# The first batch of a two-layer graph kernel: products of ones during the first loads, conv1 half by half, messages later, three x parts ahead of the way back

## The chip, the cores and the metric

The kernel runs on one core of a Trainium2 chip. The metric is the device time of one execution in microseconds (us), as a median over runs. PE is TensorE, PEld its weight load, DVE is VectorE, ACT is ScalarE, POOL is GpSimd. "L461" is a line of the kernel; the change shifts lines, so L461 of before is L465 of after, L380 is L384, L396 is L400, L521 is L538, L555 is L573, L693 is L711.

## The reference, cut to what matters

64 graphs of 256 nodes and 256 features go through two layers; all is float32.

```python
# layer 0, per graph
h = relu(bn1(conv1d(xT, conv1_w)))              # 1x1 convolution over the nodes
h = bn2(conv1d(h, conv2_w, pad=8))              # 17 taps along the nodes
x_conv = relu(h + xT).T
s = x @ w_se.T + b_se                           # 3 numbers a node
A = exp(-|s_n - s_m|^2) * adj
msg = relu(x @ w_msg.T + b_msg)
x_in = concat([x_conv, A @ msg])
# GRU: gates from x_in @ w_ih.T and x @ w_hh.T, then x = layernorm(x + gru)
# layer 1: x = layernorm(x + relu(adj @ layernorm(x) @ W_rel + ... @ W_root))
```

## The kernel before, where the change touches it

Eight graphs make a batch. While the graphs of batch b go through gates and layer 1, the convolution of batch b+1 runs in between. The first batch has nothing before it, so its convolution stands alone: conv1, building the filters, a tree of VectorE adds, eight groups of products (TensorE) with a "take" each (VectorE), and the "way back", 20 VectorE steps whose result TensorE turns. Then the first gates can start.

Some words recur. A pair is two graphs; a batch has pairs 0 to 3. The profile counts each f32 matmul as two instructions, called passes. "Turned" means transposed by TensorE. An x part is a quarter of turned x that TensorE leaves in PSUM, for a quarter of the way back to be added to it. Messages, factors, distances, mask and passing are, for one graph, the steps to A @ msg: the message matmul, the turned s, the exponential of the distances, its product with adj, and the product with the messages. A gate matmul belongs to the GRU. The clock is the share of TensorE's full speed that the profile says was granted.

```python
for g in range(0, BG, 2):                       # conv1, two graphs at a time
    xTc = conv_pool.tile([P, C, 2 * N], F32, tag="xTc", name="xTc", bufs=1)
    ...                                         # 8 transposes, 2 ScalarE copies into xTc
    nc.scalar.dma_start(out=xt_dram[pair], in_=xTc)     # the write of turned x
    for o in range(C):
        ps = bank("ps_c1")
        for c in range(C):
            nc.tensor.matmul(ps, w1[:, c, o * P:(o + 1) * P], xTc[:, c, :], ...)
...
held = [turned_x(0), turned_x(1)]               # two x parts before the way back
... for q in range(4):                          # way back, by quarters
        second(q); third(q); third(q + 4)       # VectorE
        pss = held.pop(0)                       # TensorE adds the quarter to its x part
        ...
        if q < 2: held.append(turned_x(q + 2))
...
while STAGE.get(0) != "inverse":
    if next(first) is None:                     # a product group is done
        count += 1
        if count == 2:   messages(0, True)
        elif count == 3: messages(1, True)
        elif count == 4: factors(0)
        elif count == 5: distances(0)
...
nc.gpsimd.tensor_add(brzn[:, :2 * D], brzn[:, :2 * D], bhh)
early = {1: lambda: messages(2, True), 4: lambda: mask(0), 5: lambda: factors(1)}
later = deque([lambda: distances(1), lambda: passing(0)])
```

`bank` hands out the eight PSUM banks in a ring. `xTc` has one buffer, so the copies of a pair wait until the write of the pair before has landed.

## Time and profile before

| | value |
|---|---|
| time, median of 3 runs | 2287.5 us (2286.13 to 2288.14) |
| span of the profiled run | 2289.9 us (that run took 2291.63) |
| PE busy | 2228.0 us, 97% |
| products begin (first L380) | 80.39 |
| last VectorE step of the way back ends | 157.04 |
| first gate matmul (L693) | 164.61 |

The profiled run was itself 4 us above the median.

```profile
19.87 1.07 ACT L453 COPY xTc<-ps_xTc 128x512 f32<-128x512 f32 x2 [0.15 <-DMA xt<-xTc]
```

The first pair of graphs takes 4.50 us instead of 3.70, because its first passes run at half clock. The views show a granted clock of 1.00 there, but the list of clock intervals in the packed trace begins only at 10.67, with an interval at full clock, and has nothing before it. That agrees with the spacing of the weight loads, which the prediction reads as a switch near 10.6.

### The profile page before, as it was taken

To read this page: it belongs to the slowest core of one execution; us is meant where nothing else is said; L and a number is where in the kernel's file an instruction comes from. 1 tells how busy PE (TensorE), PEld (TensorE's weight loads), DVE (VectorE), ACT (ScalarE), POOL (GpSimd) and SP (SyncE) were. 2 spreads that over 40 slices of the span, in tenths; PEclk is the share of its full clock that TensorE was granted. 3 is DMA by queue.
4 is the path that set the end of the run, shared out by engine and by line. 5 is a ranking of instruction groups with operands and counts; after the bars stand their busy time and mean duration, and the time that the engine had idled before them with its cause. 6 is when DMAs were issued, how large, how long until landed. Compare 5 with 4: busy or idle time off the path is not lost.

```text
span 2289.9 us, 24427 instructions
## 1 busy us (share of the span) xinstructions
PE 2228.0 (97%) x8370; PEld 1463.0 (64%) x8370; DVE 1678.3 (73%) x3188; ACT 768.1 (34%) x1585; POOL 464.0 (20%) x926
## 2 busy tenths in 40 slices
PE   8989999999999999999999999999999999999996
PEld 5765666666665666656666566666666566666663
DVE  6875979478882988749886597947888398874443
ACT  6423222432234322443224422243223432243332
POOL 0101212221220221213022121222122022121211
PEclk9989999999999999999999999999999999999998
DMA  5922432314422153232422243231442315321100
GB/s 146 312 92 74 130 119 83 101 51 138 134 74 101 39 170 99 75 101 93 146 85 76 83 129 120 82 102 51 138 133 74 102 39 163 102 79 37 47 23 14
DMA packets 212665, 226.68 MB, mean 99 GB/s; under 512 B 22087, under 2 KB 203838, under 8 KB 212542
## 3 DMA queue, kind: packets, MB, share of 16 engines
q1 hardware_dynamic: 189984, 191.14, 26.1%
q10 hardware_dynamic: 22558, 33.99, 4.3%
q8 instruction: 67, 1.10, 0.2%
q14 instruction: 56, 0.46, 0.1%
HBM read 179.22 MB, written 45.88 MB: 98 GB/s over the span
## 4 chain that ended last, share of the span: by engine, by line
PE 79%; DVE 14%; DMA 3%; issue 2%; POOL 1%; ACT 1%; SPq 0%; ACTq 0%; POOLq 0%; DVEq 0%
PE ps_rz L695 16%; PE ps_k L380 12%; PE ps_n L707 8%; PE ps_rz L693 8%; PE ps_out L770 7%; PE ps_c L461 5%; DVE XF L103 5%; PE ps_nmp L677 5%; PE ps_n L705 4%; PE ps_msg L627 4%; PE ps_out L782 4%; DMA w<-w2m 2%; PE ps_w L225 2%; DVE w L103 1%; DVE bst L712 1%
## 5 line engine op out<-in xcount | busy, mean ns | idle before, releaser
L103 DVE SCALAR_TENSOR_TENSOR XF<-XF 128x512 f32<-128x512 f32 (+2 forms) x800 | 508.2, 665 | 7.4
L734 POOL TENSOR_SCALAR q<-mv 128x2 f32<-128x2 f32 x64 | 32.1, 501 | 1473.6 <-DVE mv L713 1473.6
L380 PE MATMUL ps_k<-w,XF 128*128 128x256 f32 x1316 | 304.5, 387 | 15.9 <-ACT AT L667 11.6
L380 PEld LDWEIGHTS ps_k<-w,XF 128*128 128x128 f32 x1316 | 249.4, 192 | 65.6 <-ACT AT L667 17.3
L708 DVE TENSOR_TENSOR gn<-ps_n,brzn 128x512 f32<-128x512 f32 x128 | 87.9, 687 | 239.9 <-PE ps_n L707 239.9
L699 ACT ACTIVATE rz<-rz 128x512 f32<-128x512 f32 x128 | 80.7, 631 | 507.1 <-DVE rz L698 507.1
L693 PE MATMUL ps_rz<-whh,xT 128*128 128x512 f32 x512 | 240.8, 592 | 0.0
L695 PE MATMUL ps_rz<-wih,nmp 128*128 128x512 f32 x512 | 240.6, 592 | 0.0
L695 PE MATMUL ps_rz<-wih,xc 128*128 128x512 f32 x512 | 240.6, 592 | 0.0
L770 PE MATMUL ps_out<-wrr,hT 128*128 128x512 f32 x512 | 231.8, 596 | 5.5 <-ACT hT L759 5.5
L698 DVE TENSOR_TENSOR rz<-ps_rz,brzn 128x512 f32<-128x512 f32 x128 | 87.1, 680 | 199.9 <-PE ps_rz L695 199.8
L695 PEld LDWEIGHTS ps_rz<-wih,xc 128*128 128x128 f32 x512 | 97.3, 190 | 122.5 <-issue 122.2
L695 PEld LDWEIGHTS ps_rz<-wih,nmp 128*128 128x128 f32 x512 | 97.3, 190 | 122.4 <-issue 122.4
L770 PEld LDWEIGHTS ps_out<-wrr,hT 128*128 128x128 f32 x512 | 97.8, 191 | 104.5 <-issue 88.9
L638 ACT ACTIVATE msg<-msg 128x512 f32<-128x512 f32 x61 | 38.5, 631 | 335.1 <-DVE msg L636 335.1
L627 PE MATMUL ps_msg<-wms,xT 128*128 128x260 f32 x512 | 133.2, 399 | 5.8 <-DVE XF L396 4.2
L693 PEld LDWEIGHTS ps_rz<-whh,xT 128*128 128x128 f32 x512 | 92.2, 190 | 64.5 <-issue 61.2
L705 PE MATMUL ps_n<-whh,xT 128*128 128x256 f32 x512 | 131.6, 379 | 0.0
L707 PE MATMUL ps_n<-wih,nmp 128*128 128x256 f32 x512 | 131.4, 379 | 0.0
L707 PE MATMUL ps_n<-wih,xc 128*128 128x256 f32 x512 | 131.4, 379 | 0.0
L357 DVE TENSOR_TENSOR XF<-XF 128x512 f32<-128x512 f32 (+3 forms) x128 | 125.2, 1003 | 1.7
L771 ACT COPY hr<-ps_out 128x256 f32<-128x256 f32 x128 | 47.7, 373 | 229.9 <-PE ps_out L770 229.9
(115 smaller groups left out, 3556.1 us busy)
## 6 DMA issues: line engine op xcount, KB each, us to landing
w<-w2m SPq DMA_DIRECT2D x105, 768.0 KB, 5.8
xn<-in_x_dram SPq DMA_DIRECT2D x32, 512.0 KB, 4.4
xt<-xTc ACTq DMA_DIRECT2D x32, 512.0 KB, 3.2
xT<-xt SPq DMA_DIRECT2D x64, 256.0 KB, 2.9
xb<-in_x_dram SPq DMA_DIRECT2D x32, 512.0 KB, 5.3
adj<-in_adjT_dram SPq DMA_DIRECT2D x64, 256.0 KB, 2.7
x<-in_x_dram SPq DMA_DIRECT2D x64, 256.0 KB, 3.0
out_dram<-y ACTq DMA_DIRECT2D x64, 256.0 KB, 2.2
```

Of the source, the lines that this page charges most:

```text
L103: nc.vector.scalar_tensor_tensor(o, in0, s, in1, op0=op0, op1=op1)
L357: (nc.vector.tensor_add if add else nc.vector.tensor_sub)(sl(o, n), sl(a, n), sl(b, n))
L380: nc.tensor.matmul(ps, X[:, slot, c * P:(c + 1) * P], w(m, c), start=(c == 0), stop=(c == C - 1))
L461: nc.tensor.matmul(ps, w1[:, c, o * P:(o + 1) * P], xTc[:, c, :], start=(c == 0), stop=(c == C - 1))
L627: nc.tensor.matmul(ps[:, :D + 4], XT[k][:, c, m * P:(m + 1) * P], wms[:, c, :], start=(c == 0), stop=(c == C - 1 and not idle))
L677: nc.tensor.matmul(ps[:, d * N:(d + 1) * N], MSG[k][:, m, d * P:(d + 1) * P], AT[k][:, m, :], start=(m == 0), stop=(m == C - 1))
L693: nc.tensor.matmul(prz, XT[k][:, c, q], whh[:, c, 0:2 * D], start=(c == 0), stop=False)
L695: nc.tensor.matmul(prz, t, wih[:, i, 0:2 * D], start=False, stop=(i == 3))
L705: nc.tensor.matmul(pn[:, D:], XT[k][:, c, q], whh[:, c, 2 * D:], start=(c == 0), stop=(c == C - 1))
L707: nc.tensor.matmul(pn[:, :D], t, wih[:, i, 2 * D:], start=(i == 0), stop=(i == 3))
L770: nc.tensor.matmul(ps, hT[:, c, n * P:(n + 1) * P], wrr[:, c, :], start=(c == 0), stop=(c == C - 1))
L782: nc.tensor.matmul(po, ADJ[k][:, m, n * P:(n + 1) * P], hr[:, m, :], start=False, stop=(m == C - 1), skip_group_check=True)
```

## The change

The intent is to shorten the first 165 us: let TensorE reach full clock during the first loads, use each half of x as it lands, keep messages out of the way of the product group that VectorE waits for, and put work into the stretch in which VectorE alone decides.

```diff
+    warm = bank("ps_warm")
+    for _ in range(8):
+        nc.tensor.matmul(warm[:, :P], ones, ones, start=True, stop=True)
 ... conv1
+            if b == 0:
+                pss = [bank("ps_c1") for _ in range(C)]
+                for c in range(C):
+                    for o in range(C):
+                        product1(o, c)           # half of x outermost
 ... way back
-            held = [turned_x(0), turned_x(1)]
+            yield None
+            held = [turned_x(q) for q in range(3)]
-                if q < 2:
-                    held.append(turned_x(q + 2))
+                if q == 1:
+                    held.append(turned_x(3))
 ... product groups of batch 0
-            if count == 2:                       # messages(0); 3: messages(1); 4: factors(0); 5: distances(0)
+            if count == 3:                       # 4: messages(1); 5: factors(0); 6: distances(0)
+    messages(2, True)
-    early = {1: lambda: messages(2, True), 4: lambda: mask(0), 5: lambda: factors(1)}
-    later = deque([lambda: distances(1), lambda: passing(0)])
+    early = {2: lambda: factors(1), 3: lambda: mask(0), 4: lambda: passing(0)}
+    distances(1)                                 # after the way back
```

More of the change, by code (lines that the diff above doesn't have):

```diff
@@ L457, in conv, with product1 @@
             yield None
-            for o in range(C):
-                ps = bank("ps_c1")
-                for c in range(C):
-                    nc.tensor.matmul(ps, w1[:, c, o * P:(o + 1) * P], xTc[:, c, :], start=(c == 0), stop=(c == C - 1))
+            pss = []
+            def product1(o, c):
+                nc.tensor.matmul(pss[o], w1[:, c, o * P:(o + 1) * P], xTc[:, c, :], start=(c == 0), stop=(c == C - 1))
+            if b == 0:
[3 more added lines that the diff above has]
+                        product1(o, c)
+            for o in range(C):
+                if b > 0:
+                    pss.append(bank("ps_c1"))
+                    for c in range(C):
+                        product1(o, c)
+                ps = pss[o]
                 pv = ps.rearrange("p (g t j) -> p j g t", g=2, j=M)
@@ L888, in gnn_two_layers @@
             count += 1
-            if count == 2:
+            if count == 3:
                 messages(0, True)
-            elif count == 3:
+            elif count == 4:
                 messages(1, True)
-            elif count == 4:
+            elif count == 5:
                 factors(0)
-            elif count == 5:
+            elif count == 6:
                 distances(0)
+    messages(2, True)
     first_pool.close()
@@ L906, in gnn_two_layers @@
     load_x(0)
-    early = {1: lambda: messages(2, True), 4: lambda: mask(0), 5: lambda: factors(1)}
-    later = deque([lambda: distances(1), lambda: passing(0)])
-    for i, t in enumerate(first):
+    early = {2: lambda: factors(1), 3: lambda: mask(0), 4: lambda: passing(0)}
+    for i, _ in enumerate(first):
         if i in early:
             early[i]()
-        if t is None and later:
-            later.popleft()()
+    distances(1)
     mask(1)
```

## The prediction

> **What bounds the kernel now.** The page first: TensorE is busy 97% of a 2289.9 us span and carries 79% of the chain that ended last. The second view, the busy time by slices of the first 200 us, shows where it is not busy; only there can a change to the first batch gain anything.
>
> ```profile
> PE 2228.0 (97%) x8370; PEld 1463.0 (64%) x8370; DVE 1678.3 (73%) x3188; ACT 768.1 (34%) x1585; POOL 464.0 (20%) x926
> ```
>
> ```profile
> 0.00:10.00 10.00, 5.00 (x18) 4.14 (x19) 2.40 (x14) 3.04 (x4) 3.04 (x13) 1.00 0.90 231
> ...
> 130.00:140.00 10.00, 7.13 (x41) 5.67 (x39) 9.69 (x18) 0.37 (x1) 0.00 (x0) 0.85 0.82 255
> 140.00:150.00 10.00, 5.64 (x15) 3.18 (x15) 9.73 (x15) 1.72 (x6) 4.34 (x7) 0.50 0.69 217
> 150.00:160.00 10.00, 10.00 (x68) 9.47 (x68) 7.47 (x12) 4.92 (x10) 0.32 (x1) 0.80 0.01 2
> ```
>
> The columns after the window's length are PE, PEld, DVE, ACT, POOL, then granted PE clock, DMA share, GB/s. The first 200 us hold 16.9 us of TensorE's 62 idle us, in two places: the start (5 us with nothing to do), and 130 to 150 us, the "way back" of the first batch's convolution. There VectorE is full (9.7 of 10) and TensorE waits for it, at half clock for part of it.
>
> Third view, TensorE's own timeline from 84 us (start, duration, instructions, idle before):
>
> ```profile
> 92.26 1.11 PE L627 MATMUL ps_msg<-wms,xT 128*128 128x260 f32 x4 [1.11 <-issue]
> ...
> 104.23 5.45 PE L380 MATMUL ps_k<-w2all,XF 128*128 128x256 f32 x24
> 109.51 0.38 PE L653 MATMUL ps_sT<-ident,st 128*36 128x128 f32 x2
> ...
> 136.13 1.34 PE L521 MATMUL ps_xc<-ident,xb 128*128 128x128 f32 x8 [2.87 <-DVE XF L396]
> ...
> 148.53 3.96 PE L555 MATMUL ps_xc<-ident,XF 128*128 128x128 f32 x16 [3.82 <-DVE XF L103]
> 152.28 2.79 PE L521 MATMUL ps_xc<-ident,xb 128*128 128x128 f32 x16
> ...
> 161.04 3.73 PE L555 MATMUL ps_xc<-ident,XF 128*128 128x128 f32 x32
> 164.61 1.88 PE L693 MATMUL ps_rz<-whh,xT 128*128 128x512 f32 x4
> ```
>
> And VectorE's, same stretch:
>
> ```profile
> 101.19 0.69 DVE L396 TENSOR_TENSOR XF<-XF,ps_k 128x512 f32<-128x512 f32 x1 [1.68 <-PE ps_k L380]
> ...
> 109.78 0.69 DVE L396 TENSOR_TENSOR XF<-XF,ps_k 128x512 f32<-128x512 f32 x1 [5.06 <-PE ps_k L380]
> ...
> 145.14 11.90 DVE L103 SCALAR_TENSOR_TENSOR XF<-XF 128x512 f32<-128x512 f32 x18
> ```
>
> Read together: up to 109.78 VectorE waits for TensorE (5.06 us) because two message steps stand between product groups. From 109.78 on it never waits until its last way-back step ends at 157.04 (145.14 + 11.90): 47.3 us of unbroken work. TensorE then still has 7.6 us queued before the first gate matmul at 164.61. So the path is TensorE to 109.7, VectorE to 157.0, TensorE after that; from 164.6 on TensorE is nearly full to the end, so what is gained before it should reach the end whole. The printed chain hangs the stretch from 133 on a DMA; VectorE was busy all through it, so I do not follow the chain there.
>
> **What the Trainium skill says.** "TensorE: Matmul & The Clock Gate", Part 1: the array starts and falls back to half clock, and goes to full clock only after a busy window of about 3.4 us, free-running, so the switch moves from run to run. The trace agrees: the weight loads of the first L461 are 0.86 us apart (8.85, 9.71, 10.56), then 0.43, so the switch came near 10.6, 5.6 us after the first matmul (the recorded clock reads 1.00 there, which the spacing contradicts); the clock fell to 0.50 at 137.0 after a 2.87 us gap, and came back at 154.0, 17.0 us later, five windows of 3.4. The same page, "Why this matters for your kernels", advises no gaps above about 3 us. "SBUF — State Buffer", "Who interferes with whom": VectorE reading two SBUF operands and a GpSimd read lock each other out. The trace agrees: one L103 step at 142.87 took 1.75 us against 0.69 for its neighbours while GpSimd's L905 add ran 142.39 to 144.07. That add stays. "PSUM — Partial Sum Buffer", "The four PSUM rules": eight banks; three x parts held in advance take six, so later users wait for a bank's reader.
>
> **The change part by part.**
>
> (1) Eight products of ones. Added: 8 matmuls 128x128 f32, two passes each. A cold pass of 128 columns is 0.21 us: L461's cold pass of 512 columns takes 0.86, a quarter of that. So 16 x 0.21 = 3.4 us. They wait only for the memset of ones (ends 1.02), so they run 1.1 to 4.5, before the first x lands at 4.86 (the chain has that load 0.73 + 4.14): they cost nothing. Gain: with 0.4 us of pause the clock should rise at a window edge in about 4.5 to 8 us instead of 10.6. L461 of the first pair then saves its two slow steps, 0.86 us; L161 is partly held by VectorE's dg tiles and saves about 0.5. Sum 1.4. It may be damped by DMA, which is full to 18.6 us and whose xt write at 15.41 took 4.38 and releases the tile of pair 2.
>
> (2) conv1 half by half. Same matmuls. The first half's result is complete after the third matmul, not the second, so ScalarE's two evictions start 0.86 later; they end just as the second half's could start (2.57 + 0.2 + 1.0 against 3.43 + 0.2). In before the second matmul never waited for the second copy (copies 0.5 apart, matmul 0.86). So it buys nothing and may cost 0.07 a pair, 0.2 in all. With the damping I take 1.1 net for (1) and (2).
>
> (3) Messages later. Messages(0) moves from after product group 1 to after group 2, messages(1) after group 3, messages(2) after group 7. The 1.11 us before messages(0) is its xT load (issued from 83.35, 7.0 us to land): one group later, 5.4 us, it is there, gain 1.1. And only one message step (92.26 to 95.64, 3.3 us) is left before the end of group 3, which releases VectorE at 109.78. So that release moves by 1.1 + 1.1 + 3.3 = 5.5, to 104.3. VectorE is free by then: group 2's take, now at about 98.3 (its merges end 99.51 - 1.1), plus the 3.5 us from 101.19 to 104.72, gives 101.8. Later takes are never ahead of their groups: groups 4 to 7 end by about 112.7, 118, 123.8, 128.4, the takes come at 119, 122.6, 129.9, 133.3. VectorE's end: 157.04 - 5.5 = 151.5.
>
> (4) Three x parts ahead, passing(0) before, distances(1) after the way back. In before, after VectorE's end TensorE still ran part of its queue to 164.61, 7.6 us. Now TensorE ends the products at 128.4, messages(2) at 131.7, three x parts (48 passes x 0.107 = 5.2) at 136.9, and passing(0) once mask(0) is done (137.4) at 139.1. It then waits to 143.0 (148.5 - 5.5) for the first quarter: 3.9 us, enough for the clock to fall. From there a quarter is ready each 2.85 us (148.5 to 157.04 in three). Work: two quarters, the fourth x part, two quarters, distances: 5 x 1.75 + 0.63 warm. Never cold: 151.5 + 1.75 + 0.63 = 153.9. Cold for 3.4 to 6.8 us: 154.3 to 155.6. I take 154.7. From VectorE's end to the gates is then 3.2 instead of 7.6: gain 4.4. ScalarE's relu of the last quarter (four of 0.46) ends about 156, when the whh gate matmuls (1.72) have just run: no stall.
>
> Sum: 1.1 + 1.1 + 3.3 + 4.4 = 9.9 us; first gate matmul at 154.7 instead of 164.6; 2287.5 - 9.9 = 2277.6.
>
> **Rivals.** (a) The clock rules: if the warm products do not lift it (the windows may need more than 88% busy), part 1 gives 0; a bad phase in the way back costs 1 more. Total gain 7.5 to 8.5: 2279 to 2280. For: in before a window about two thirds busy did not lift it. (b) The later work comes due elsewhere: passing(1), distances(1) or loads become the wait after 155, since adjacency, wih and x start only 2.2 us earlier (they wait for the last product) while the gates start 9.9 earlier. Against: wih landed about 8.5 us after its issue, at 140.6; now about 138.5, with the gates at 156; and pair loads have 10 us of room. If half is lost: 2282. (c) The bank ring: the second half of the third x part waits for the take of group 7 (about 133.5, needed 136), the fourth x part for the readers of passing and factors. Small room, but none on VectorE's path; at worst 1 us. (d) More: before also loses to cold windows in 137 to 154, and if TensorE keeps its clock the gain is nearer 11.5: 2276.
>
> **Range and chances.** The terms are uncertain by about 0.8, 0.3, 0.5 and 1.2, and two executions of one kernel differ by 2 us here[...]. So 2272.5 to 2282.5. 2% is 46 us, more than the whole idle time of the first 200 us, so faster by 2% is out of reach; slower would need a stall that the order does not show.
>
> **What would show it.** Right: L461's weight loads 0.43 apart from the first pair; no 1.1 us gap before messages(0); VectorE's 5.06 us wait cut to about 2.5 and its way back ending near 151.5; the first L693 near 154.7; from there equal spacing. Wrong: L461 still 0.86 apart; VectorE waiting inside 104 to 151; a gap of several us before the gates' wih matmuls; or a first gate at 155 with an end that moved less.

## More of the kernel before

The views that bound the kernel stand in the prediction. Two more matter later: TensorE's timeline of conv1 (start, duration, instructions, and in brackets the idle time before them with what ended it) and one line of ScalarE's.

```profile
8.85 4.50 PE L461 MATMUL ps_c<-xTc,w 128*128 128x512 f32 x8
...
14.94 3.70 PE L461 MATMUL ps_c<-xTc,w 128*128 128x512 f32 x8 [0.71 <-ACT xTc L453]
...
20.51 3.70 PE L461 MATMUL ps_c<-xTc,w 128*128 128x512 f32 x8 [0.99 <-ACT xTc L453]
```

The copies of pair 2 waited only 0.15 us for the write of turned x: the write was just about hidden.

## The result and the profile after

The changed kernel took 2278.97 us (median of 6 runs, 2275.36 to 2282.39); the kernel before took 2287.49 (6 runs, 2285.87 to 2288.14) in the same rounds. The ratio is 0.9964, 95% interval 0.9951 to 0.9977. A ratio is the mean time of one kernel's runs over that of the other's of the same rounds, so it is not quite the ratio of the medians. The outputs were correct.

The page's line of engines, and the busy times by slices in the form that the prediction uses (after the length: PE, PEld, DVE, ACT, POOL, granted PE clock, DMA share, GB/s):

```profile
PE 2224.9 (98%) x8386; PEld 1462.9 (64%) x8386; DVE 1678.0 (74%) x3188; ACT 766.9 (34%) x1585; POOL 467.1 (20%) x926
```

```profile
0.00:10.00 10.00, 8.10 (x35) 6.71 (x36) 2.35 (x14) 3.04 (x4) 3.04 (x13) 1.00 0.89 224
130.00:140.00 10.00, 10.00 (x68) 8.21 (x67) 9.69 (x20) 1.98 (x7) 1.78 (x5) 1.00 0.89 280
140.00:150.00 10.00, 6.59 (x30) 6.06 (x29) 9.79 (x15) 2.87 (x6) 1.63 (x2) 0.66 0.60 195
150.00:160.00 10.00, 10.00 (x68) 7.87 (x67) 3.31 (x6) 6.27 (x14) 0.32 (x1) 1.00 0.18 52
```

TensorE is now full from 130 to 140 (before 7.13) at full clock (before 0.85), and VectorE is done at the beginning of the last slice, where it was still busy before. From 140 to 150 the clock is low again. Next, TensorE's timeline of the start, and ScalarE's line that goes with it:

```profile
1.07 3.79 PE L136 MATMUL ps_warm<-ones 128*128 128x128 f32 x16 [1.07 <-DVE ones L132]
...
8.79 3.60 PE L465 MATMUL ps_c<-xTc,w 128*128 128x512 f32 x8
...
14.03 3.70 PE L465 MATMUL ps_c<-xTc,w 128*128 128x512 f32 x8 [0.76 <-ACT xTc L457]
...
20.62 3.70 PE L465 MATMUL ps_c<-xTc,w 128*128 128x512 f32 x8 [2.02 <-ACT xTc L457]
```

```profile
19.98 1.07 ACT L457 COPY xTc<-ps_xTc 128x512 f32<-128x512 f32 x2 [1.14 <-DMA xt<-xTc]
```

The products of ones lie where they were meant to, and the first pair runs at full clock (3.60 instead of 4.50), so pair 1 starts 0.91 us earlier. The list of clock intervals begins at 6.59 here; it begins at 3.98 to 7.29 in all ten profiles with the ones and at 10.08 to 12.53 in the four without. But the copies of pair 2 now wait 1.14 us for the write of turned x, and pair 2 starts at 20.62, where before it started at 20.51: all is given back. The first pair did not even begin earlier (8.79 against 8.85), because the small load of the norm factors, on which the row products ahead of it hang, landed at 4.12 instead of 3.41. Now the middle and the end, TensorE first and then VectorE:

```profile
81.00 15.94 PE L384 MATMUL ps_k<-w2all,XF 128*128 128x256 f32 x72
96.79 1.04 PE L645 MATMUL ps_msg<-wms,xT 128*128 128x260 f32 x4
...
133.00 5.62 PE L538 MATMUL ps_xc<-ident,xb 128*128 128x128 f32 x48
...
138.76 2.00 PE L695 MATMUL ps_nmp<-AT,msg 128*128 128x256 f32 x8
144.17 6.67 PE L573 MATMUL ps_xc<-ident,XF 128*128 128x128 f32 x32 [3.41 <-DVE XF L103]
150.68 1.95 PE L538 MATMUL ps_xc<-ident,xb 128*128 128x128 f32 x16
152.46 3.74 PE L573 MATMUL ps_xc<-ident,XF 128*128 128x128 f32 x32
...
156.76 1.98 PE L711 MATMUL ps_rz<-whh,xT 128*128 128x512 f32 x4
```

```profile
105.65 0.69 DVE L400 TENSOR_TENSOR XF<-XF,ps_k 128x512 f32<-128x512 f32 x1 [2.22 <-PE ps_k L384]
...
138.62 14.06 DVE L103 SCALAR_TENSOR_TENSOR XF<-XF 128x512 f32<-128x512 f32 x20
```

Three product groups run without a break (81.00 to 96.8), and messages(0) follows with no idle time before it. VectorE waits 2.22 us instead of 5.06 for group 3 and ends its way back at 152.68 (138.62 + 14.06). From there to the first gate it is 4.08 us instead of 7.57. The first gate is 7.85 us earlier than before. The gap of 3.41 us before the first quarter costs the clock: the 32 passes that follow take 6.67 us, the same 32 passes at full clock 3.74. Not all of this difference is the clock: the second quarter also waits for VectorE, and where the clock stayed up (filled gap, below) these passes spread over 5.1 us.

Last, one thing that later batches show in the same timeline of TensorE. Each later batch starts with the same 20 passes after the same wait:

```profile
289.88 4.58 PE L384 MATMUL ps_k<-w,XF 128*128 128x256 f32 x20 [1.12 <-ACT AT L685]
...
1917.54 6.27 PE L384 MATMUL ps_k<-w,XF 128*128 128x256 f32 x20 [1.12 <-ACT AT L685]
```

At 1918.1, half a microsecond into the passes, the clock fell and they took 1.7 us longer; at 290 it did not. Which of the batch starts are hit differs from run to run. Each such fall lasts 3.4 us in the recorded clock, and the fourteen profiles hold none to four of them between the first gate and 2200 us. The two profiles without any need 2120.7 us on average from the first gate to the end, the three with three falls 2123.9; but of the six with one, two need 2123.3 and 2123.5. So the falls go with a part of the spread between single runs of one kernel, which reaches 8 us; that they are all of it is not shown. Because of this spread the experiments are judged by the stages of their profiles first and by their times second.

### The profile page after: what moved, and what is told of

Same layout as the page of the kernel before. It is cut to its first block, busy times and chain, and to the rows that moved or that the text cites. A ratio compares the mean times of both kernels' runs of the same rounds, so it can differ in the third digit from the quotient of the medians. Undisturbed runs are those within 1.5% of the kernel's fastest.

```text
span 2278.7 us, 24459 instructions
## 1 busy us (share of the span) xinstructions
PE 2224.9 (98%) x8386; PEld 1462.9 (64%) x8386; DVE 1678.0 (74%) x3188; ACT 766.9 (34%) x1585; POOL 467.1 (20%) x926
## 4 chain that ended last, share of the span: by engine, by line
PE 76%; DVE 17%; issue 2%; DMA 2%; POOL 1%; ACT 1%; ACTq 0%; SPq 0%; POOLq 0%; DVEq 0%
PE ps_rz L713 16%; PE ps_k L384 10%; PE ps_n L725 8%; PE ps_rz L711 8%; PE ps_out L788 7%; DVE XF L103 6%; PE ps_c L465 5%; PE ps_nmp L695 4%; PE ps_n L723 4%; PE ps_out L800 4%; PE ps_msg L645 4%; DVE w L103 1%; DMA w<-w2m 1%; DVE XF L361 1%; DVE bst L730 1%
```

## The experiments

Twelve runs were made (one of them of the changed kernel, unaltered), each correct, each in rounds with the kernel before. This table holds what their profiles show; "tail" is from VectorE's end to the first gate, "rest" is the span less the time of the first gate.

| kernel | filters begin | products begin | VectorE ends | first gate | tail | rest |
|---|---|---|---|---|---|---|
| before | 29.34 | 80.39 | 157.04 | 164.61 | 7.57 | 2125.3 |
| after | 29.49 | 81.00 | 152.68 | 156.76 | 4.08 | 2121.9 |
| after, again | 29.07 | 80.19 | 151.88 | 155.10 | 3.22 | 2120.1 |
| no ones | 30.06 | 81.18 | 152.84 | 155.91 | 3.07 | 2123.7 |
| old conv1 order | 29.82 | 80.90 | 152.56 | 155.67 | 3.11 | 2123.2 |
| second tile | 28.32 | 79.44 | 151.11 | 154.13 | 3.02 | 2120.9 |
| second tile, no ones | 30.48 | 81.58 | 153.23 | 156.49 | 3.26 | 2123.5 |
| late filter load | 29.35 | 80.47 | 152.13 | 156.15 | 4.02 | 2121.4 |
| start alone | 31.05 | 82.17 | 158.46 | 165.36 | 6.90 | 2123.2 |
| messages alone | 29.31 | 80.37 | 152.18 | 160.15 | 7.97 | 2124.5 |
| messages back | 29.03 | 80.14 | 155.60 | 159.63 | 4.03 | 2121.0 |
| filled gap | 28.86 | 79.97 | 151.63 | 154.13 | 2.50 | 2120.4 |
| bias on VectorE | 29.35 | 80.45 | 151.15 | 153.94 | 2.79 | 2123.3 |
| three together | 28.16 | 79.28 | 150.00 | 152.49 | 2.49 | 2121.0 |

From filters to products it is 51.1 us in all but one of them; in the recorded profile of after it is 51.5. There a GpSimd scaling began at 73.52 beside the VectorE step that scales a filter, and that step took 1.48 us instead of 0.65.

### No ones

```diff
-    warm = bank("ps_warm")
-    for _ in range(8):
-        nc.tensor.matmul(warm[:, :P], ones, ones, start=True, stop=True)
```

> The changed kernel without the eight products of ones. My theory (loads set the start: the copy of x parts for pair 2 waits for the write of turned x, whenever TensorE is ready): the weight loads of the first pair's L465 group (a few lines earlier here) are again 0.86 us apart until about 10.6, pair 1 starts about 0.9 later than 14.03, but pair 2 still starts at about 20.6 and the first filter group (tT) at 29.5 +- 0.4; first gate at 156.8 +- 0.5 and the time within 2 us of the changed kernel's 2279. Rival (the products of ones do gain their 1.1 to 1.4 us): pair 2, the filters and the first gate each 1.1 to 1.4 us later.

Measured: 2278.31 us (4 runs; before 2287.23), ratio 0.9961. TensorE's timeline:

```profile
9.61 4.52 PE L462 MATMUL ps_c<-xTc,w 128*128 128x512 f32 x8
...
21.18 3.70 PE L462 MATMUL ps_c<-xTc,w 128*128 128x512 f32 x8 [0.83 <-ACT xTc L454]
...
30.06 1.04 PE L204 MATMUL ps_tT<-ident,ws 128*119 128x128 f32 x8
```

The first pair runs at half clock again, and pair 1 comes 1.74 us later than in after (15.77), not the 0.9 that I expected. At the filters 0.57 us of that is left, so the ones are worth a little more than my theory said (29.5 +- 0.4 expected, 30.06 measured) and less than the rival's 1.1, by that one profile. But the recorded profile of after was a late one: against the mean of the five profiles with the whole change's start (29.16) it is 0.90, which is nearer to the rival. This run alone does not decide between the two. The first gate came outside my range, but on the early side (155.91): the half-clock stretch of the way back was shorter in this run. Without the ones the wait for the write was gone: pair 2 was late for its own reasons.

### Old conv1 order

```diff
-            if b == 0:
+            if False:
```
(and the old loop for every batch)

> The changed kernel with the first batch's conv1 in its old order, half of outputs by half of outputs. My theory (the order is worth nothing, as predicted at 0 to -0.2): conv1 of the first batch ends within 0.2 us of the changed kernel's, the first gate at 156.8 +- 0.4. Rival (the new order pays because each half of x is used as it lands): conv1 ends 0.5 us or more later.

Measured: 2279.69 us (4 runs; before 2287.23), ratio 0.9964. The filters begin 0.33 us later than in after, outside my 0.2, but the order is not the reason. Busy times by slices show that the clock, which rose at 4.4 us, fell again:

```profile
7.00:8.00 1.00, 0.55 (x4) 0.55 (x4) 0.58 (x5) 0.00 (x0) 0.06 (x1) 0.92 1.25 226
8.00:9.00 1.00, 1.00 (x5) 0.74 (x5) 0.55 (x2) 0.00 (x0) 0.00 (x0) 0.50 1.32 226
```

The granted clock (third column from the end) goes to 0.50 at 7.8, after TensorE had been busy for 12% of the slice from 6 to 7 and 55% of the next, and the first pair takes 4.55 us. A pair that waits for nothing but its own copies gives the clean comparison: 5.28 us here (pair 1, transposes at 13.73 to the next at 19.01), 5.34 with the new order (pair 1 of the next experiment, 12.29 to 17.63). So the new order costs 0.06 us a pair, and the prediction's estimate was 0.07.

### Second tile of turned x

```diff
-            xTc = conv_pool.tile([P, C, 2 * N], F32, tag="xTc", name="xTc", bufs=1)
+            if b == 0 and g % 4 == 2:
+                xTc = FIRST["pool"].tile([P, C, 2 * N], F32, tag="xTc2", name="xTc", bufs=1)
+            else:
+                xTc = conv_pool.tile([P, C, 2 * N], F32, tag="xTc", name="xTc", bufs=1)
```

> The changed kernel with a second tile of turned x for every other pair of the first batch, so that no copy waits for the write of the pair before. My theory (the start gain was eaten by that wait): the 1.1 us wait before the copies of pair 2 is gone, pair 2 starts 1.3 to 2 us earlier than 20.6 and the first filter group near 28.0 to 28.5, unless the load of x for the later pairs becomes the wait (then 0.5 us or less is gained and the wait stands in the lines as one on the x load). Rival (something else holds conv1, such as TensorE's own work): the filters start within 0.2 us of 29.5 with no DMA wait in front.

Measured: 2278.09 us (4 runs; before 2287.23), ratio 0.9959. TensorE's timeline:

```profile
8.86 3.60 PE L468 MATMUL ps_c<-xTc,w 128*128 128x512 f32 x8
...
19.44 3.70 PE L468 MATMUL ps_c<-xTc,w 128*128 128x512 f32 x8 [0.77 <-ACT xTc L460]
...
28.32 1.04 PE L207 MATMUL ps_tT<-ident,ws 128*119 128x128 f32 x8
```

As the theory has it: pair 2 starts 1.18 us earlier (I expected 1.3 to 2), with only the usual 0.77 us for the copies before it, and the filters begin at 28.32. Against the means of the five profiles (20.29 and 29.16) both come 0.8 us earlier. No x load takes the wait's place. The start gain was there and stood behind the write.

### Second tile, no ones

> The kernel with the second tile of turned x, without the products of ones: asks what the ones are worth when the write of turned x no longer stands in the way. With that wait and the ones, the first filter group began at 28.32. Theory A (the clock gain is real, 0.9 to 1.7 us, and only hidden behind the write in the changed kernel): it now begins at 29.2 to 30.0. Theory B (the ones do nothing, since the clock comes up by itself): 28.3 +- 0.3. Without the ones the first pair's weight loads should be 0.86 us apart until about 10.6.

The edit is the second tile together with the removal of the ones. Measured: 2278.89 us (4 runs; before 2287.67), ratio 0.9964. TensorE's timeline:

```profile
9.53 5.09 PE L465 MATMUL ps_c<-xTc,w 128*128 128x512 f32 x8
...
30.48 1.04 PE L204 MATMUL ps_tT<-ident,ws 128*119 128x128 f32 x8
```

Theory A, and more than it said: without the wait for the write the ones are worth 30.48 - 28.32 = 2.16 us in this pair of profiles, 0.67 before the first pair (9.53 against 8.86) and 1.49 in it (5.09 against 3.60). It is an upper end: in the four profiles without the ones the first pair took 4.16 to 5.09 us.

### Start alone

The kernel before with the ones and the new conv1 order, nothing else.

> The kernel before with the products of ones and the half by half order alone. Asks two things. (1) In all eight kernels with the new way back the first small load (the norm factors) landed 0.65 to 0.75 us later than in the two without it, with or without ones. If that belongs to the way back (or to where code and data lie), it lands at 3.4 here; if to the ones or the order, at 4.1. (2) With an early landing, the first pair's conv1 begins near 8.2 and ends 1.5 us earlier than before's; theory (the write of turned x then holds pair 2): first filter group still at 28.8 to 29.5 (before 29.34), products at 79.9 to 80.5, first gate 164.2 to 164.8, time within 2 us of before. Rival (the start's gain of 1.1 arrives, as I predicted): filters at 28.2, first gate at 163.5.

Measured: 2287.45 us (4 runs, 2283.5 to 2290.4; before 2288.13), ratio 0.9991, interval 0.9975 to 1.0006. TensorE's timeline:

```profile
14.00 3.70 PE L464 MATMUL ps_c<-xTc,w 128*128 128x512 f32 x8 [0.77 <-ACT xTc L456]
...
20.48 5.40 PE L464 MATMUL ps_c<-xTc,w 128*128 128x512 f32 x8 [1.90 <-ACT xTc L456]
```

Pair 2 started at 20.48, as the theory says. Then something came that neither had: half a microsecond into pair 2, after the idle time made by the wait (1.90 us), the clock fell, pair 2 took 5.40 us, and the filters began 1.7 us later than before. The recorded clock confirms it (0.95 from 20.5 to 21, 0.50 from 21 to 24). In after TensorE was idle for 2.02 us at the same place and the clock stayed at 1.00, so the length of the idle time alone does not decide. The small load landed at 4.09, so its delay is not tied to the way back. Of the twelve profiles that hold the ones or the new order, eleven have it at 3.87 to 4.20 and only the late filter load below has it early, at 3.46, like the two with neither (3.41 and 3.50). Why a load that is issued at the same 0.72 us lands 0.7 us later stays open.

### Late filter load

```diff
         fetch(0)
-        fetch(1)
         yield
         ...
+        fetch(1)
         TT[0] = turned(WS[0], 4)
```

> The changed kernel with the second 714 KB load of conv2 filters issued behind conv1's own loads instead of at the start: the other way to the same cause. Theory (the write of turned x is slow because it shares full DMA engines with that load): writes of turned x land in 4.5 us or less instead of 5.0 to 5.4, pair 2's copies wait 0.3 us or less for DMA instead of 0.5 to 1.1, the first filter group starts at 28.2 to 28.6 (28.9 to 29.5 in five runs of the changed start), and the late load is not missed: products begin at 79.3 to 80.3. Rival (the write takes 5 us whatever else moves): filters at 28.9 or later; or the late load stalls the filters, and products begin after 81.

Measured: 2280.57 us (4 runs; before 2289.73), ratio 0.9966. TensorE's and ScalarE's timelines:

```profile
13.38 3.70 PE L465 MATMUL ps_c<-xTc,w 128*128 128x512 f32 x8 [0.77 <-ACT xTc L457]
...
20.47 3.70 PE L465 MATMUL ps_c<-xTc,w 128*128 128x512 f32 x8 [2.52 <-ACT xTc L457]
```

```profile
19.83 1.07 ACT L457 COPY xTc<-ps_xTc 128x512 f32<-128x512 f32 x2 [1.63 <-DMA xt<-xTc]
```

My expectation failed. The small load landed early, and pair 1 started at 13.38, but the copies of pair 2 waited 1.63 us, until 19.83. The edit did not test what it was made for: the load was issued at 13.06, just ahead of the write at 13.84, and so shared the engines with it in the very stretch that should have been free (DMA share 1.02 to 1.18 from 17 to 20, where in after it is down to 0.60 and 0.06 from 18 to 20). What it does show is useful: a write issued at 13.84, at 14.2 to 14.5 (after and its kin) or at 15.16 and 15.41 (messages alone and before) releases the tile at 19.35 to 19.98 in every run in which the copies waited for it. An earlier issue bought nothing. Whether contention with loads alone is the reason stays open.

### Messages alone

The kernel before with the four counts moved from 2, 3, 4, 5 to 3, 4, 5, 6.

> The kernel before, with messages(0), messages(1), factors(0) and distances(0) each put off by one group and nothing else of the change. My theory: VectorE's take of group 3 comes at about 105.4 instead of 109.78 (no 1.1 us gap before messages(0), one message step fewer before group 3), its way back ends at about 152.6, and the way from there to the first gate stays near 7.6 us: first gate near 160.2, 4.4 earlier than before, and a time about 4 us under the kernel before (2283), half of the whole gain. Rival (the later messages come due in the way back and push the gate): VectorE's end moves 4 us but the gate less than 2.

Measured: 2284.13 us (4 runs; before 2287.23), ratio 0.998, interval 0.9961 to 0.9999. VectorE's line of the take of group 3, and TensorE's end:

```profile
105.01 0.69 DVE L396 TENSOR_TENSOR XF<-XF,ps_k 128x512 f32<-128x512 f32 x1 [1.94 <-PE ps_k L380]
```

```profile
143.67 3.96 PE L555 MATMUL ps_xc<-ident,XF 128*128 128x128 f32 x16 [7.03 <-DVE XF L103]
...
160.15 1.88 PE L693 MATMUL ps_rz<-whh,xT 128*128 128x512 f32 x4
```

All of the theory's events came within 0.5 us: take at 105.01, VectorE's end at 152.18 (4.86 earlier), first gate 4.46 earlier, tail 7.97. In the times 3.1 of it is seen.

### Messages back

The changed kernel with the counts back at 2, 3, 4, 5.

> The changed kernel with the first two message steps, factors and distances back at their old places and everything else of the change kept. Theory (the parts add: messages 4.4, the rest only shortens the way from VectorE's end to the gates): take of group 3 at 109.5 to 110.5 instead of 105.65, VectorE's way back ends at 156.5 to 157.5, way from there to the first gate 3.0 to 4.1, first gate 160 to 161, time 3.5 to 4.5 us above the changed kernel's and about 4 under the kernel before. Rival (the later messages were only a precondition of the new order in the way back, no gain of their own): first gate within 2 us of 156.8.

Measured: 2281.83 us (4 runs; before 2287.67), ratio 0.9975. VectorE, then TensorE:

```profile
108.43 0.69 DVE L400 TENSOR_TENSOR XF<-XF,ps_k 128x512 f32<-128x512 f32 x1 [5.06 <-PE ps_k L384]
```

```profile
147.08 6.63 PE L573 MATMUL ps_xc<-ident,XF 128*128 128x128 f32 x32 [2.72 <-DVE XF L103]
...
159.63 1.98 PE L711 MATMUL ps_rz<-whh,xT 128*128 128x512 f32 x4
```

The 5.06 us wait of before is back, word for word, and the tail is short (4.03). VectorE's end, the take and the gate came about 1 us earlier than I had it, because the 1.11 us gap before messages(0) is not there in this run. (In "start alone", which also has the old order, it is 0.72 us: the gap changes from run to run.) The two parts add roughly: first gate 4.46 earlier by messages alone, 4.98 by the rest, 9.4 together, against 7.85 and 9.51 in the two profiles of the whole change. The gap is gone in both runs, so this sum counts it twice; with it counted once the sum is 8.3.

### Filled gap

```diff
             early[i]()
+        if i == 4:
+            fill = bank("ps_fill")
+            for _ in range(14):
+                nc.tensor.matmul(fill[:, :P], ones, ones, start=True, stop=True)
```

> The changed kernel with 14 products of ones (6 us at half clock, 3 at full) after passing(0), in the gap where TensorE waits for the first quarter of the way back. Theory (the half clock in 141 to 150 costs the last term 0.6 to 1.0 us, depending on where its windows fall): the granted clock stays at 1.00 through 140 to 155, the first gate comes 2.5 us after VectorE's end (3.1 to 4.1 in the four runs with the change so far), so near 155.2; and no more than 1.5 us of the whole time. Rival (the fill runs over into the first quarter, or its bank makes the x part wait): first gate 156.5 or later.

Measured: 2280.23 us (4 runs, 2276.29 to 2281.65; before 2287.67), ratio 0.9966. TensorE's timeline:

```profile
139.53 3.29 PE L934 MATMUL ps_fill<-ones 128*128 128x128 f32 x28
143.12 2.43 PE L573 MATMUL ps_xc<-ident,XF 128*128 128x128 f32 x16 [0.30 <-DVE XF L103]
...
154.13 1.98 PE L711 MATMUL ps_rz<-whh,xT 128*128 128x512 f32 x4
```

The clock stayed at 1.00, the quarters wait for VectorE instead of running late, and the tail is 2.50 us, as expected. The gate came at 154.13 rather than 155.2, because the start had been 1 us earlier. The times do not show the gain.

### Bias on VectorE

The add of the two gate biases moves from GpSimd, in the way back, to VectorE after it.

```diff
-    nc.gpsimd.tensor_add(brzn[:, :2 * D], brzn[:, :2 * D], bhh)
     load_x(0)
     ...
     distances(1)
+    nc.vector.tensor_add(brzn[:, :2 * D], brzn[:, :2 * D], bhh)
```

> The changed kernel with the add of the two gate biases (brzn) moved from GpSimd, where it runs during VectorE's way back, to VectorE behind it. Theory (that add blocks one VectorE step, 1.75 instead of 0.69 us, and that lies on the path): the 20 steps of the way back take 13.0 instead of 14.06 us, VectorE's end and the first gate 1.0 us earlier at the same clock, and the moved add (under 1 us) costs nothing. Rival (the slow step has another cause, such as the DMA traffic of that stretch): still 14.0.

Measured: 2281.26 us (4 runs; before 2287.67), ratio 0.9972. VectorE's timeline:

```profile
138.05 13.10 DVE L103 SCALAR_TENSOR_TENSOR XF<-XF 128x512 f32<-128x512 f32 x20
151.07 0.68 DVE L931 TENSOR_TENSOR brzn<-brzn,bhh 128x512 f32<-128x512 f32 x1
```

The 20 steps take 13.10 instead of 14.06 us and the moved add 0.68 where VectorE is idle: the theory holds. The first gate is at 153.94. Again the four times do not show it.

### After, again, and three together

The changed kernel unaltered, and the changed kernel with the second tile, the bias on VectorE and a fill of 10 products, in the same five rounds.

> The changed kernel once more, unaltered, on another chip and in the same rounds as the two below. Theory (its profile on record was an unlucky draw: products begun at 81.00, where the same start began at 79.97 to 80.45 in three other runs; first quarters of the way back 1 us longer at half clock than in four others): products begin at 80.0 to 81.0, the first gate at 155.0 to 156.8, median 2277 to 2281, runs 3 us or more apart. Rival (the draw was typical): products at 81.0, first gate at 156.8, both within 0.2.

> Three repairs on top of the changed kernel: the second tile of turned x, the bias add on VectorE behind the way back, and 10 products of ones in the gap after passing(0). If they add: products begin near 79.5, VectorE's way back (1.0 shorter) ends at 150.1 to 150.4, first gate 2.5 later at 152.6 to 152.9, that is 3 to 4 us before the changed kernel's; median 2 to 5 us under the changed kernel of the same rounds (run above). Rival (what is gained before the first gate is lost again behind it, in waits or in falls of the clock): first gate as said, but median within 1 us of the changed kernel.

Measured: after again 2280.96 us (5 runs, 2275.43 to 2282.36), ratio 0.9962; three together 2278.59 (5 runs, 2275.24 to 2280.7), ratio 0.9957; before 2288.13 (9 runs). TensorE's timeline of the repeat, then of the three:

```profile
143.37 5.81 PE L573 MATMUL ps_xc<-ident,XF 128*128 128x128 f32 x32 [3.44 <-DVE XF L103]
...
155.10 1.98 PE L711 MATMUL ps_rz<-whh,xT 128*128 128x512 f32 x4
```

```profile
144.14 2.43 PE L576 MATMUL ps_xc<-ident,XF 128*128 128x128 f32 x16 [0.23 <-DVE XF L103]
...
152.49 1.98 PE L714 MATMUL ps_rz<-whh,xT 128*128 128x512 f32 x4
```

The draw of the recorded profile was unlucky, as my theory had it: the repeat has its products 0.81 earlier, the half-clock passes 0.86 shorter and the first gate at 155.10. In the eleven runs of the changed kernel in both sets of rounds, five took 2275.4 to 2277.5 and six 2280.4 to 2282.4.

The three repairs do add up to the first gate: 152.49, 2.6 us before the repeat's. What reaches the end is not settled. The median is 2.4 us lower, the mean 1.2 (2278.3 against 2279.5), and the intervals of the ratios (0.9944 to 0.9969, 0.9949 to 0.9975) overlap. In these two profiles the lead went from 2.61 at the first gate to 0.73 at the last, in steps of both signs at the starts of the later batches, and the spans differ by 1.7; between the two profiles of the unaltered kernel the difference went from 1.66 to 4.36 in the same way, and the spans differ by 3.5. So median and mean speak for the version with the three repairs, but these runs do not prove it faster.

## Why the prediction was right or wrong

The time on record was 2277.6 with 2272.5 to 2282.5; the median came at 2278.97 and 2280.96 in the repeat. The reading of the bound was right: TensorE to the take of group 3, VectorE to the end of its way back, TensorE after it. One reading of the profile was not: the two places that the prediction names for TensorE's 16.9 idle us hold 12.2 of them, and 2.4 of the others lie from 10 to 30 us, where the pairs of conv1 wait for their copies. The terms:

**The start, steps (1) and (2): predicted 1.1 net, measured nothing.** This is the term that failed. Five profiles with the whole changed start (after, again, messages back, filled gap, bias on VectorE) begin their products at 79.97 to 81.00, on average at 80.35; two with the old start (before, messages alone) at 80.38. A sixth with the changed start, "start alone", begins them at 82.17, because its clock fell; with it the average is 80.65. The part about the clock was right (in after it had risen by 6.59, within the 4.5 to 8 us that were expected), and its worth rather too modest (2.16 us in the one pair of profiles where nothing stands in its way). The step that failed is "With the damping I take 1.1 net". I had named the write as a damper and given it a fraction. In these runs it acted not as a damper but as a floor: it released the tile at 19.35 to 19.98 in every run in which the copies waited, whatever TensorE had gained before it, and before already waited there for the last 0.15 us, hence no room. The second tile shows that this wait held the gain; why the write lands when it does stays open. The small load landed late too: the first pair began at 8.13 where it was early (late filter load) and at 8.79 in after, so about 0.7 us of the gain was gone ahead of the write, for a reason that stays open. For step (2), whose cost was put at up to 0.07 a pair, the measured 0.06 agrees.

**The messages, step (3): predicted 1.1 + 3.3 = 4.4, measured 5.0.** From products to VectorE's end it was 76.65 us before and 71.68 in after (71.69 in the repeat), so 4.97. The gap before messages(0) is gone, one message step fewer stands before group 3, and the two experiments on messages confirm it from both sides (messages alone, messages back). The 1.1 for the gap is the less certain part: in "messages back" it was gone with the old order too, and from products to VectorE's end that run needs 75.46 us, only 3.8 more than after. That VectorE would not be held again between 104 and 151 was right.

**The tail, step (4): predicted 7.6 to 3.2, measured 7.57 to 4.08 in the recorded profile.** Over the eight profiles with this tail unaltered it lies between 3.02 and 4.08, on average 3.48, so the gain is 4.1 instead of 4.4. The mechanism was right, the fall of the clock included: the gap was 3.41 us (I had 3.9), and the variant "never cold", which I worked out at 1.75 + 0.63 = 2.4 us after VectorE's end, measured 2.50 when the gap was filled. The size goes with how long the clock stays down, which changes from run to run: in the recorded clock it was down for 3.4 us in the five of these profiles with tails of 3.02 to 3.26, and for 6.8 us or more in the three with 4.02 to 4.08. The prediction had allowed for both. Of the pieces of step (4), such as the third x part ahead or the place of passing, none was tested alone.

**The sum: predicted 9.9 at the first gate, measured 7.85** in the recorded profile (-0.61 + 4.97 + 3.49) and 9.51 in the repeat (0.20 + 4.96 + 4.35). In the times it is 8.5 and 7.2 by medians, and the ratios 0.9964 and 0.9962 of 2287.5 make 8.2 and 8.7. The time is met more closely than its terms: the start's missing 1.1 was partly made up by the 0.6 that the messages gave beyond their 4.4, and this was luck. The total also lies in the 7.5 to 8.5 of rival (a), but not for its reason, since the products of ones did lift the clock. And the 2 us that the prediction allows between two executions of one kernel were too few: the six runs of after alone lie 7 us apart.

**"What is gained before it should reach the end whole".** The rest, from first gate to end, is 2120 to 2125 us in all fourteen profiles, without a trend with the gate for kernels of the new way back. The three kernels of the old way back need 2.5 us more on average (2124.3 against 2121.9), but their profiles hold three or four falls of the clock there and the others none to three, so this is no sure gain of the change. So rival (b), later work that comes due elsewhere, is not seen on average; but a gain of 1 or 2 us at the gate drowns in that spread. Rival (a), the clock, made the tail of the recorded profile 0.9 longer than predicted. Rival (c), the bank ring, was not seen in after (the three x parts run through, 133.00 to 138.6); in "messages back" the third part waited 0.84 us for a reader of VectorE. (The page that the prediction cites for the eight banks, "PSUM — Partial Sum Buffer", states them in its section "PSUM: the matmul accumulator".) Rival (d) did not come, since TensorE never kept its clock by itself.

## What to carry to other kernels

A gain of speed ahead of a buffer is worth only the slack of what releases that buffer: look at the wait of the consumer in the profile of before, and if it is near zero, count the gain as zero until the release is moved too. Where one engine decides a stretch, order the other engine's work by what that engine waits for, and put the free work into its gaps; here that was worth eight to nine microseconds at the first gate with no work removed. When single runs spread by more than the effect, compare named events within the profiles and repeat the profile, rather than add rounds.

## What the Trainium skill lacked or had wrong

- "TensorE: Matmul & The Clock Gate", "Why this matters for your kernels", warns of gaps above about 3 us. Here shorter ones sufficed in some runs: 1.90 us before pair 2 in "start alone" (5.40 us instead of 3.70 for the same eight passes), and 1.12 us at the start of a later batch (6.27 instead of 4.58 for the same 20 passes of one profile); yet 2.02 us before pair 2 in after left the clock at 1.00. So the row's figure is no safe limit. The page does tell elsewhere of short idles that made the clock swing in another kernel, but gives no length for them.
- The same page, Part 1, says that the switch moves from run to run. It has no figure for what this does to a tuned kernel with several short gaps: here none to four falls of 3.4 us came after the first gate, and the eleven runs of one kernel lie between 2275.4 and 2282.4 us, a spread wider than what each part of this change is worth (how much of it is the clock is not shown). It also has no case in which a clock won by a burst of products during the loads is lost before the real work: with the old conv1 order it rose at 4.4 us and was at 0.50 from 7.8 on.
- No page that I found tells why the first small load lands at 3.4 us in some of these programs and at 3.9 to 4.2 in others, though it is issued at 0.72 in both, nor why a write of 512 KB lands near the same time (19.35 to 19.98) whether it is issued at 13.84 or at 15.41.
